# A graph layer on one core: other weights for the dense steps when they are dealt over the groups

## The chip, the cores and the metric

The kernel runs on one core of a Trainium2 chip. The metric is device time in microseconds (us), a median over runs; a profile of one execution stands beside it. TensorE (PE) multiplies, VectorE (DVE) and ScalarE (ACT) work elementwise, GpSimd (POOL) issues the indirect DMAs that gather rows, SyncE (SP) issues the plain DMAs.

## What is computed

The reference, cut to what matters:

```python
def reference(x, src, dst, edge_type_4, W, b):      # x 12500x128, 200000 edges, W 4x128x128
    h = jnp.maximum(layernorm(x), 0.0)
    xs = h[src]
    msgs = zeros
    for i in range(4):
        msgs += jnp.where(edge_type == i, xs @ W[i] + b[i], 0.0)
    return x + jax.ops.segment_sum(msgs, dst, num_segments=12500)
```

The edges come sorted by `dst`, and the low nodes have many more edges than the high ones.

## The kernel before

The edges are taken in chunks of 128. The first 568 chunks (`C0`), whose nodes have many edges, are the **dense part**; the rest is the **grouped part**, groups of 16 chunks (`G`), numbered from 0, 65 in all.

*Preparation.* The table of normalised rows, each as three 16-bit parts (768 bytes), is written to `htab` in device memory. Meanwhile the first three groups (`RAW = 3`, the "raw groups") gather rows of x itself, since the table isn't there yet, and normalise them on ScalarE.

*A group of the grouped part* (3 and up). POOL gathers the rows of each chunk from `htab` (`gather`, L591), two chunks to a buffer `hm`, ten buffers. VectorE makes a one-hot matrix of each chunk (`one_hots_of`, L609). `sum_up` multiplies rows by one-hots (L644), a pair of chunks, called a part, at a time, eight parts to a group; ScalarE evicts the sums (L634). `weigh` multiplies by the weights (L670) in the second part of the next group, and VectorE adds the result to a ring of output columns (`ring_adds`, L733).

*The dense part* has 19 batches of up to 31 units of three nodes. `count` counts, for each batch, how often each table row goes to each node: one matmul of two one-hot matrices for each slot (L1099), 1069 slots in all; VectorE makes both one-hots (L1066, L1074), ScalarE casts the result to integers (L1107). `multiply` then passes the whole table by those counts, 33 steps of three blocks of 128 rows: a load of `hs` by SP, and matmuls (L1211). The first batch's pass reads `htab`, uses all three parts of a row (nine matmuls a step), and writes the rows again, in a shorter form, to `dtab` (`keep`, L1181 and L1182, stores from ScalarE's queue). The later passes read `dtab` and have six matmuls a step; three of them take counts that ScalarE has decoded to floats (L1167). While one batch is passed, the next one is counted. Two stretches of counting stand alone: that of the first batch, where there is nothing to pass yet, and the first half of the third one's (`SETTLE = 0.5`), which goes ahead of the second batch's pass.

*The order.* From group 3 on, the order on TensorE, VectorE and ScalarE is the program's own. Ahead of each part of a group, the loop pulls steps from the generator `dense_work` until the share of dense work done, `spent`, has reached what is due by then:

```python
while work and spent < pace(gi, part):
    spent = next(work, None)
```

`pace` wants groups of equal length: each group, from 3 to 58, gets the same number of columns in all, its own (`columns`) and dense ones. `dense_columns` is the sum of dense columns that it reckons with, and `dense_work` has a weight for each batch's counting and pass, from which it works out `spent`. In both, a node of a pass costs `PARTS` = 2.05 times 392 columns, in the first pass 3.0 times. A slot is 392 columns; in the first batch `dense_work` makes it 3.5 times that, `dense_columns` does not. In the first of the groups from 3 on the 20 steps of the raw groups' products stand as well (`raw_steps`), which no column count has in it.

Of the kernel before, what the change touches and what calls it, by code (L numbers as in the profile page):

```python
# [66 lines left out]
SETTLE = 0.5  # L67
# [5 lines left out]
LEAD = RAW  # L73
# [4 lines left out]
DECS = 4  # L78
UP = 4096.0
PARTS = 2.05  # L80


@with_exitstack
def kernel(
# [13 lines left out]
    NT, _, DO = w.shape  # L98
    assert D == P and DO == P
    NW = -(-N // P)  # L100
# [19 lines left out]
    def chunks_of(d, n):  # L120

        m = E * (((d + n) / N) ** 0.5 - (d / N) ** 0.5)
        return max(1, -(-int(m + ODDS * m**0.5) // P))
# [18 lines left out]
    for k in range(max(segs[0][4])):  # L142
        for s in (0, 1, 2, 3) if k == 0 else (1, 0, 2, 3):
            n = sum(c > k for c in segs[s][4])
# [11 lines left out]
    def window_of(c):  # L156

        m = min((c - C0) // G, FULL)
        end = (C0 + (m + 1) * G if m < FULL else T) * P / E
        a_node = E * ((end**2 + 1 / N) ** 0.5 - end)  # L160
        return next((n for n in range(8, WIN, 2) if (n - 1) * a_node > P + 5 * P**0.5), WIN)
# [6 lines left out]
    alone = [(k, d) for k in range(0, max(segs[0][4]), 2) for d in range(FIRST) if segs[0][4][d] > k]  # L168
# [10 lines left out]
    batches = []  # L179
# [11 lines left out]
    def slot_at(k, d):  # L191
        s = next(s for s in (3, 2, 1, 0) if d >= segs[s][2])
        return blocks[k, s][0] + (d - segs[s][2]) // segs[s][3]

    def slots_of(u):

        got = []
        u = list(zip(u, (1.0, 256.0, 65536.0)))
        if u[0][0] is not None and u[0][0][1] >= FIRST:
            d = u[0][0][1]  # L200
            size = size_of(d)
            got += [(slot_at(k, d), None) for k in range(chunks_of(d, size))]
            del u[:size]
        for v, by in u:
            if v is not None:
                k, d = v
                got += [(slot_at(i, d), by) for i in (k, k + 1) if i < segs[0][4][d]]
        return got

    NSLOTS = sum(len(slots_of(u)) for vs in batches for u in vs)  # L210
    NB = NW * NT
# [132 lines left out]
    def prep_steps(m, prep):  # L344
        c0, c1 = C0 + m * P, min(C0 + (m + 1) * P, T)
        got = []
        for name, of, rest in (("si", src, 0), ("ty", etype, NT), ("di", dst, N - 1)):
            t = prep.tile([P, 1, P], I32, name=name)
            edge_rows(t, of, c0, c1, rest)
            got.append(t)  # L350
        load_brow(m)
        si, ty, di = got
        if c1 > NFULL and REST:
            r = (NFULL - c0) % P
            nc.sync.dma_start(di[r : r + 1, 0, REST:], dst[E - (P - REST) :].rearrange("(p e) -> p e", p=1))
        yield 0
        sf = prep.tile([P, 1, P], F32, name="sf")
        nc.vector.tensor_copy(sf, si)
        nc.vector.tensor_copy(head[:, m : m + 1], di[:, :, 0])
        rel = prep.tile([P, 1, P], F32, name="si")  # L360
        nc.vector.tensor_scalar(rel[:, 0, :], di[:, 0, :], head[:, m : m + 1], None, ALU.subtract)
        key = prep.tile([P, 1, P], F32, name="di")
        nc.vector.scalar_tensor_tensor(
            key[:, 0, :], ty[:, 0, :], span[:, m : m + 1], rel[:, 0, :], op0=ALU.mult, op1=ALU.add
        )
        nc.vector.tensor_reduce(ends[:, m : m + 1, 0], rel, AX.X, ALU.max)
        nc.vector.tensor_sub(ends[:, m : m + 1, 0], ends[:, m : m + 1, 0], span[:, m : m + 1])
        nc.vector.tensor_reduce(ends[:, m : m + 1, 1], rel, AX.X, ALU.min)
        yield 1
        settle(owed)  # L370
        pg = x_ps.tile([P, 2, P], F32, name="pt")
        nc.tensor.transpose(pg[:, 0, :], sf[:, 0, :], ident)
        nc.tensor.transpose(pg[:, 1, :], key[:, 0, :], ident)
        nc.scalar.copy(srcT[:, m % TURN, :], pg[:, 0, :])
        nc.scalar.copy(keyT[:, m % TURN, :], pg[:, 1, :])
# [240 lines left out]
    def settle(of):  # L616
        while of:
            of.pop(0)()
# [642 lines left out]
    def columns(gi):  # L1261

        K = NT * window_of(C0 + starts[gi])
        return sizes[gi] * (3 * max(64, K) + 5 * K)

    def pace(gi, part):

        last = FULL - 1
        if gi >= last:
            return 2.0  # L1270
        own = [columns(i) for i in range(LEAD, last)]
        a_group = (dense_columns() + sum(own)) / len(own)
        n = gi - LEAD
        if n < 0:
            return 0.0
        return ((n + part) * a_group - sum(own[:n]) - part * own[n]) / dense_columns()

    def dense_columns():
        return NSLOTS * float(NB) + sum(3 * len(vs) * (PARTS if i else 3.0) for i, vs in enumerate(batches)) * NW * NT

    def begin(n):
        now = [batches[n], None]
        return now, count(now, lambda: rooms[n % 2])

    def dense_work():


        a_slot = float(NB)
        alone_slot = 3.5 * NB
        a_node = NW * NT  # L1290
        total = dense_columns() + sum(len(slots_of(u)) for u in batches[0]) * (alone_slot - a_slot)
        gone = 0.0
        before = None
        coming = None
        for n, vs in enumerate(batches + [None]):
            steps, led = {}, {}
            now = None
            if n == 1:
                end_raws()
            if vs:  # L1300
                now, first = coming or begin(n)
                coming = None
                steps[first] = sum(len(slots_of(u)) for u in vs) * (a_slot if before else alone_slot)
            if before:
                passed = multiply(before)
                steps[passed] = 3 * len(before[0]) * a_node * (PARTS if before[0] is not batches[0] else 3.0)
                led = {passed: SETTLE if before[0] is batches[1] else BEHIND}
            done = {st: 0.0 for st in steps}
            opened = 0 if before else DECS - 1
            while done:  # L1310
                while opened < DECS - 1 and (
                    vs is None or done.get(first, 1.0) >= led[passed] - BEHIND * (DECS - 1 - opened) / (DECS - 1)
                ):
                    next(passed)
                    opened += 1
                st = min(done, key=lambda st: done[st] + led.get(st, 0.0))
                part = next(st, None)
                if part is None:
                    del done[st]
                    gone += steps[st]  # L1320
                    if vs and st is first and n + 1 < len(batches):
                        coming = begin(n + 1)
                        next(coming[1])
                else:
                    done[st] = part
                    yield (gone + sum(done[st] * steps[st] for st in done)) / total
            before = now
        settle(sds)

# [98 lines left out]
    for gi, us in enumerate(group_of):  # L1428
# [9 lines left out]
        for i, u in enumerate(us):  # L1438
# [7 lines left out]
            last = None  # L1446
            for l in more_looks[:each]:
                last = l()
# [50 lines left out]
    def end_raws():  # L1499

        while raw_steps:
            raw_steps.pop(0)()
        if len(rooms) > 1:
            return
        raw_sums = outp.tile([P, OT, D], F32, name="xo").rearrange("p j d -> p (j d)")[:, : raw_at[-1]]
        nc.scalar.copy(raw_sums, raw_py[:, : raw_at[-1]])
        for m in range(RAW):
            win = window_of(C0 + m * G)
            of = lambda i, m=m, win=win: raw_sums[:, raw_at[m] + i * win : raw_at[m] + (i + 1) * win]
            raw_adds.append(ring_adds(m * G, G, of, win))  # L1510
        raw_room.close()
        rooms.append(counting.enter_context(tc.tile_pool(name="dense2", bufs=1)))
        rooms.append(counting.enter_context(tc.tile_pool(name="hsp", bufs=STREAM, side="right")))

    work = dense_work()

    gates.extend(ties + marks[len(marks) - (20 - 1 - len(ties)) :])

    steps = [prep_steps(1, later)]
# [11 lines left out]
    for gi, (t0, g) in list(enumerate(zip(starts, sizes)))[RAW:]:  # L1531
        q = (t0 + 8 * G) // P
        if (t0 + 8 * G) % P < G and 2 <= q < BM:
            steps = [prep_steps(q, later)]
# [17 lines left out]
        for j, part in enumerate(sum_up(t0, g, *now, gi >= FULL)):  # L1552
            late, tails[:] = list(tails), []
            while work and spent < pace(gi, part):
                spent = next(work, None)
                if spent is None:
                    work = None
# [80 lines left out]
    with tc.If(rv > 0):  # L1638
        with tc.tile_pool(name="slow", bufs=1) as slow, tc.tile_pool(name="slow_ps", bufs=1, space=PSUM) as slow_ps:
# [10 lines left out]
            before = slow.tile([P, P], F32, name="before")  # L1650
# [108 lines left out]
```

## Time and profile before

| | |
|---|---|
| median of 3 runs | 1355.36 us (1352.13 to 1356.22) |
| the profiled execution | 1360.44 us |
| its span | 1358.7 us |
| PE busy | 1243.1 us (91%) |
| ACT busy | 1066.8 us (79%) |
| DVE busy | 999.0 us (74%) |
| POOL busy | 977.8 us (72%) |
| gathers by POOL (L591) | 947, mean 976 ns |

In the rows of the prediction, a group of instructions reads: line, engine, operation, out<-in, count, busy time and mean ns of one, idle time before them and what ended it. A row by stretches has the stretch, then busy time and count of each engine, then TensorE's granted clock, the busy share of the DMA engines, and GB/s. A wait reads: who waited, for whom, us in total, times, the longest.

### The profile page before, as it was taken

The page shows a single profiled execution, that of the slowest core. Times are in us where ns is not written, and L with a number is a line of the kernel's source. Part 1 is how long each engine was busy: PE and PEld are TensorE (multiplying, and loading weights), DVE is VectorE, ACT ScalarE, POOL GpSimd, SP SyncE. Part 2 cuts the span into 40 slices and gives each one's busy share as a digit, 9 for nine tenths or more (in the row PEclk, how much of TensorE's full clock was granted, in tenths as well). Part 3 has the DMA queues.
Part 4 walks back from the last instruction along what each step waited for, and adds up shares of the span by engine and source line. Part 5 has one row for each costly group of instructions (what it writes and reads, how often), then busy time and mean ns, then how long its engine had stood idle before and what let it go on. Part 6 is the DMA issues. An engine that isn't in the chain of part 4 may idle for free.

```text
span 1358.7 us, 30461 instructions
## 1 busy us (share of the span) xinstructions
PE 1243.1 (91%) x9232; PEld 872.8 (64%) x9232; DVE 999.0 (74%) x5139; ACT 1066.8 (79%) x1815; POOL 977.8 (72%) x1024
## 2 busy tenths in 40 slices
PE   5888877999999999999999999999999999998964
PEld 1445654777677766777777676666676666666743
DVE  8996568868888897888776867677676758773552
ACT  6887544889889888898988988888897978886710
POOL 7637463777777777777777777777777777777774
PEclk8885887999999999999999999999999999999977
DMA  7653596888788888888888888887877878778842
GB/s 243 216 204 86 176 338 216 244 272 266 243 256 259 250 255 241 249 257 265 256 259 254 267 249 257 248 246 246 273 227 238 265 214 261 235 234 281 267 122 62
DMA packets 184630, 322.56 MB, mean 237 GB/s; under 512 B 30243, under 2 KB 82524, under 8 KB 184460
## 3 DMA queue, kind: packets, MB, share of 16 engines
q1 hardware_dynamic: 132716, 214.63, 49.0%
q0 software_dynamic: 46992, 96.30, 26.0%
q10 hardware_dynamic: 4752, 9.64, 1.8%
q8 instruction: 73, 1.20, 0.4%
q14 instruction: 97, 0.79, 0.2%
HBM read 294.78 MB, written 25.67 MB: 236 GB/s over the span
## 4 chain that ended last, share of the span: by engine, by line
PE 65%; DMA 12%; DVE 6%; ACT 6%; issue 6%; POOL 4%; DVEq 0%; SPq 0%; ACTq 0%; POOLq 0%
PE pa L1211 35%; PE pt L1099 9%; PE py L670 7%; DMA hm<-htab,srcT 7%; PE ps L644 5%; POOL hm L591 4%; DMA dtab<-dec 2%; DMA hs<-dtab 2%; ACT dec L1167 2%; PE pt L1235 2%; ACT counts L1107 1%; PE ps L702 1%; DVE o L1074 1%; DVE o L1066 1%; PE pt L952 1%
## 5 line engine op out<-in xcount | busy, mean ns | idle before, releaser
L591 POOL DMA_INDIRECT hm<-htab,srcT x947 | 924.3, 976 | 342.1 <-issue 202.5
L1167 ACT ACTIVATE dec<-counts 128x1116 fp32r<-128x1116 uint8 (+1 forms) x594 | 672.2, 1152 | 9.9 <-PE pa L1211 9.0
L1066 DVE TENSOR_SCALAR o<-iota_n,hkT 128x392 bf16<-128x392 f16 x1069 | 354.4, 331 | 180.2 <-PE pt L1099 177.4
L1211 PE MATMUL pa<-dec,hs 128*128 128x372 f32 x1764 | 480.8, 380 | 0.0
L1211 PE MATMUL pa<-counts,hs 128*128 128x372 fp8e4 (+1 forms) x2058 | 435.0, 324 | 22.6 <-DMA hs<-htab 13.8
L1211 PEld LDWEIGHTS pa<-dec,hs 128*128 128x128 f32 x1764 | 309.5, 188 | 41.6 <-issue 0.5
L1107 ACT CAST counts<-pt 128x396 int32<-128x396 f32 x580 | 285.5, 510 | 50.1 <-PE pt L1099 26.2
L1099 PE MATMUL pt<-o,o 128*128 128x396 bf16 x1069 | 285.9, 342 | 15.8 <-ACT counts L1107 9.5
L1211 PEld LDWEIGHTS <-hs 128*128 128x128 f16 (+1 forms) x2058 | 189.6, 98 | 143.1 <-issue 19.4
L644 PE MATMUL ps<-oh,hm 128*128 128x72 bf16 (+7 forms) x2841 | 186.9, 201 | 32.3 <-DMA hm<-htab,srcT 30.9
L1074 DVE TENSOR_SCALAR o<-iota,loT,byT 128x128 bf16<-128x128 bf16 x647 | 216.3, 334 | 0.0
L733 DVE TENSOR_TENSOR ring<-ring,py 128x18 f32 (+6 forms) x912 | 159.0, 174 | 73.1 <-PE py L670 24.1
L644 PEld LDWEIGHTS <-hm 128*128 128x128 f16 x2841 | 136.9, 100 | 103.9 <-DMA hm<-htab,srcT 41.4
L634 ACT ACTIVATE sb<-ps 128x288 f32<-128x288 f32 (+8 forms) x237 | 101.8, 430 | 126.3 <-PE py L670 101.3
L609 DVE TENSOR_SCALAR oh<-iota_b,keyT 128x72 bf16<-128x72 bf16 (+7 forms) x947 | 163.0, 260 | 25.6 <-PE ps L644 24.4
L670 PE MATMUL py<-sb,wsb 128*128 128x288 f32 (+6 forms) x456 | 121.1, 409 | 0.0
L1099 PEld LDWEIGHTS <-o 128*128 128x128 bf16 x1069 | 80.4, 99 | 60.6 <-issue 17.5
L1074 DVE TENSOR_SCALAR o<-iota,loT 128x128 bf16<-128x128 bf16 x422 | 116.7, 277 | 0.0
L670 PEld LDWEIGHTS py<-sb,wsb 128*128 128x128 f32 x456 | 83.3, 193 | 20.7 <-issue 0.3
L575 POOL DMA_INDIRECT hx<-in_x_dram,srcT x48 | 48.0, 1001 | 23.8 <-issue 9.5
L665 ACT CAST cnt<-pt 128x288 bf16<-128x288 f32 (+10 forms) x62 | 25.5, 412 | 39.5 <-PE pt L661 33.6
L509 ACT ACTIVATE h<-hm,nmrt,rstdt 128x128 f32<-128x128 f32 x98 | 42.1, 489 | 0.9 <-DVE mvt L492 0.8
(250 smaller groups left out, 717.8 us busy)
## 6 DMA issues: line engine op xcount, KB each, us to landing
hs<-dtab SPq DMA_DIRECT2D x576, 288.0 KB
hm<-htab,srcT POOLq DMA_INDIRECT x947
htab<-h SPq DMA_DIRECT2D x32, 288.0 KB
hs<-htab SPq DMA_DIRECT2D x32, 288.0 KB
dtab<-dec ACTq DMA_DIRECT2D x32, 288.0 KB
xo<-in_x_dram SPq DMA_DIRECT2D x23, 256.0 KB
out_dram<-xo SPq DMA_DIRECT2D x23, 256.0 KB
hm<-in_x_dram SPq DMA_DIRECT2D x18, 192.0 KB
```

The source lines that it names most:

```text
L591: one = nc.gpsimd.indirect_dma_start(out=hm[:, (i - h0) * D3 : (i - h0 + 1) * D3], out_offset=None, in_=htab, in_offset=bass.IndirectOffse ...
L609: nc.vector.tensor_scalar(oh[:, i, :], iota_b[:, :K], keyf[:, at : at + 1], None, ALU.is_equal)
L634: nc.scalar.activation(sb[0][:, i0:i1].rearrange("p g t n -> p g (t n)"), ps[:, : i1 - i0, :], AF.Copy, scale=1.0 / UP)
L644: nc.tensor.matmul(ps[:, i - i0, :], rows(i, c), oh[:, i, :], start=(c == 0), stop=(c == 2))
L670: nc.tensor.matmul(py[:, :g, :], wsb[:, t, :], sb[0][:, :g, t, :], start=False, stop=(t == NT - 1))
L733: nc.vector.tensor_tensor(to, to, of(i), ALU.add)
L1066: one = nc.vector.tensor_scalar(o2[:, k, :NB], iota_n, hkT[:, s : s + 1], None, ALU.is_equal)
L1074: one = nc.vector.tensor_scalar(o1[:, k], iota_1, loT[:, s : s + 1], by, ALU.is_equal, ALU.mult)
L1099: one = nc.tensor.matmul(pb, o1, o2, start=first, stop=last)
L1107: lambda i=i, pb=pb: nc.scalar.copy(counts[:, :, i * NT : (i + 1) * NT], pb.rearrange("p (b t) -> p b t", t=NT))
L1167: nc.scalar.activation(decoded[n][:, : j1 - j0, :nv].rearrange("p j (m v) -> p j m v", m=3), by_digit[:, j0:j1, : nu * NT * 4].rearrange(" ...
L1211: nc.tensor.matmul(to if c == 1 and not first else to.rearrange("p (m v) -> p m v", m=3), left, right, start=(j == 0 and c == 0), stop=(js ...
```

## The change

Three weights are added, and the same functions now give them to `pace` and to `dense_work`. A slot that is counted alone is charged `ALONE` = 3.5 times its columns, in the first batch and in the first half of the third, in both places. A node of the first pass is charged 4.4 times 392 columns in place of 3.0. The first group of the loop is charged 20000 columns on top of its own, some 6900, for the raw groups' products. The sum of dense columns goes from 1841890 to 1933481. What is computed, and by which instructions, stays as it is: only the places at which dense steps are pulled move.

```diff
+FIRST_PASS = 4.4
+ALONE = 3.5
+RAW_WORK = 20000.0
...
-        own = [columns(i) for i in range(LEAD, last)]
+        own = [columns(i) + (RAW_WORK if i == LEAD else 0.0) for i in range(LEAD, last)]
         a_group = (dense_columns() + sum(own)) / len(own)
...
+    def counting_columns(n, part):
+        alone = 1.0 if n == 0 else SETTLE if n == 2 else 0.0
+        return sum(len(slots_of(u)) for u in batches[n]) * NB * (part + (ALONE - 1.0) * min(part, alone))
+
+    def passing_columns(n, part):
+        return 3.0 * len(batches[n]) * (PARTS if n else FIRST_PASS) * NW * NT * part
+
     def dense_columns():
-        return NSLOTS * float(NB) + sum(3 * len(vs) * (PARTS if i else 3.0) for i, vs in enumerate(batches)) * NW * NT
+        return sum(counting_columns(n, 1.0) + passing_columns(n, 1.0) for n in range(len(batches)))
...
-        a_slot = float(NB)
-        alone_slot = 3.5 * NB
-        a_node = NW * NT
-        total = dense_columns() + sum(len(slots_of(u)) for u in batches[0]) * (alone_slot - a_slot)
+        total = dense_columns()
...
-                steps[first] = sum(len(slots_of(u)) for u in vs) * (a_slot if before else alone_slot)
+                steps[first] = lambda part, n=n: counting_columns(n, part)
...
-                steps[passed] = 3 * len(before[0]) * a_node * (PARTS if before[0] is not batches[0] else 3.0)
+                steps[passed] = lambda part, n=n: passing_columns(n - 1, part)
...
-                    yield (gone + sum(done[st] * steps[st] for st in done)) / total
+                    yield (gone + sum(steps[st](done[st]) for st in done)) / total
```

More of the change, by code (lines that the diff above doesn't have):

```diff
@@ L1319, in dense_work @@
                     del done[st]
-                    gone += steps[st]
+                    gone += steps[st](1.0)
                     if vs and st is first and n + 1 < len(batches):
```

## The prediction

> **What bounds the kernel now.** I read the page first, then the stretches of the span by engine, then the waits of POOL in two windows, then TensorE's timeline for the places where each group's result is made.
>
> ```profile
> PE 1243.1 (91%) x9232; PEld 872.8 (64%) x9232; DVE 999.0 (74%) x5139; ACT 1066.8 (79%) x1815; POOL 977.8 (72%) x1024
> L591 POOL DMA_INDIRECT hm<-htab,srcT x947 | 924.3, 976 | 342.1 <-issue 202.5
> ```
>
> The 947 gathers of the table's rows all go through POOL, and "issue" before them is no wait for anything. POOL's gathers by stretch (POOL busy with count, granted clock, DMA share, GB/s), then its waits from 250 to 1225 us (first two rows) and from 100 to 250 us (last three; us in total, times, longest):
>
> ```profile
> 95.00:245.00 150.00, 87.28 (x85) 0.74 0.62 203
> 245.00:1345.00 1100.00, 836.99 (x863) 0.98 0.81 246
> 1289.00:1345.00 56.00, 42.39 (x45) 0.71 0.40 106
> POOL hm L591 <- issue: 161.9, 531, 0.3
> POOL hm L591 <- PE pt L1099: 18.0, 59, 0.3
> ...
> POOL hm L591 <- PE ps L644: 25.1, 10, 5.0
> POOL hm L591 <- PE pt L1099: 12.4, 9, 3.4
> POOL hm L591 <- ACT sb L634: 5.7, 1, 5.7
> ```
>
> From 245 us on POOL issues without a stop: 1100 / 863 = 1.275 us a gather, no wait over 0.3 us; 16 gathers of a group make 20.4 us. Before 245 us it issued 85 gathers in 150 us, which at 1.275 would have taken 108: there it stood still for 42 us, blocked by buffers that TensorE had not freed. So POOL sets the end, but the time was lost early. TensorE is hardly less full (columns: PE, PEld, DVE, ACT, POOL, clock, DMA share, GB/s):
>
> ```profile
> 112.00:152.00 40.00, 33.32 (x200) 25.66 (x200) 21.41 (x96) 30.36 (x84) 23.69 (x25) 0.63 0.26 72
> 152.00:184.00 32.00, 24.47 (x221) 18.33 (x220) 23.01 (x104) 15.09 (x37) 19.34 (x19) 0.87 0.94 321
> 184.00:212.00 28.00, 22.81 (x206) 16.58 (x203) 17.84 (x79) 12.26 (x29) 17.24 (x18) 0.96 0.97 329
> 212.00:238.00 26.00, 19.24 (x102) 10.29 (x103) 23.48 (x113) 13.57 (x28) 9.07 (x9) 0.66 0.54 179
> 286.10:730.00 443.90, 435.00 (x3472) 315.26 (x3470) 363.99 (x1894) 393.78 (x623) 338.41 (x347) 1.00 0.84 253
> 730.00:1289.00 559.00, 536.73 (x4063) 382.13 (x4062) 390.32 (x2037) 467.53 (x712) 424.86 (x441) 1.00 0.82 251
> PE ps L644 <- DMA hm<-htab,srcT: 12.0, 21, 2.5
> ```
>
> The last row is a wait from 730 to 1290 us. From 286 to 730 us TensorE idles 8.9 us of 444 (2.0%) and never for a gathered row: it is the bound there, and POOL's lead of up to 20 gathers (ten buffers of two) is used up. From 730 on it idles 4.0%, 12 us of it for rows: POOL leads no more. Three early stretches are worse: 152 to 212 us has the DMA engines at 94 to 97%, 212 to 238 us has VectorE at 23.5 of 26 us with TensorE at 0.66 of its clock. The groups' ends (the product with the weights, made in the second pair of the next group; the first five are rows of TensorE's timeline with start and length, the sixth of the chain) show it:
>
> ```profile
> 156.21 1.49 PE L670 MATMUL py<-sb,wsb 128*128 128x192 f32 x8
> 187.01 1.49 PE L670 MATMUL py<-sb,wsb 128*128 128x192 f32 x8
> 215.42 2.17 PE L670 MATMUL py<-sb,wsb 128*128 128x192 f32 x8
> 247.70 1.49 PE L670 MATMUL py<-sb,wsb 128*128 128x192 f32 x8
> 266.57 1.49 PE L670 MATMUL py<-sb,wsb 128*128 128x192 f32 x8
> 286.11 1.34 PE py L670 x8
> ```
>
> Groups 3 to 8 end there: groups 4, 5 and 6 take 30.8, 28.4 and 32.3 us against POOL's 20.4; 7 and 8 take 18.9 and 19.5.
>
> **The change part by part.** No instruction is added or removed; only which slot countings ("counts", L1099) and which products of three node blocks ("steps", L1211) stand in which group. Counted in the two programs:
>
> ```
> group            3   4   5   6   7   8  | 9-28   29-55  (mean)
> counts before   29  12  13  41  24   4  | 22.8   18.1
> counts after    14  19   9  10  10  27  | 23.2   18.9
> steps  before    2  13  13   8  12  15  | 11.35  11.0
> steps  after     0   6  10  10   7   0  | 12.0   11.6
> ```
>
> At the end of group 8 the kernel is 34 counts and 30 steps further behind than before. All first-pass steps (33) are done by then in both. Prices (timeline rows of TensorE; group rows of VectorE; DMA):
>
> ```profile
> 206.97 2.60 PE L1211 MATMUL pa<-counts,hs 128*128 128x264 fp8e4 x18
> 249.35 0.66 PE L1211 MATMUL pa<-counts,hs 128*128 128x372 fp8e4 x3
> 250.36 0.51 PE L1099 MATMUL pt<-o,o 128*128 128x396 bf16 x2
> 250.71 0.66 PE L1211 MATMUL pa<-counts,hs 128*128 128x372 fp8e4 x3
> L1066 DVE TENSOR_SCALAR o<-iota_n,hkT 128x392 bf16<-128x392 f16 x1069 | 354.4, 331 | 180.2 <-PE pt L1099 177.4
> L1074 DVE TENSOR_SCALAR o<-iota,loT,byT 128x128 bf16<-128x128 bf16 x647 | 216.3, 334 | 0.0
> L609 DVE TENSOR_SCALAR oh<-iota_b,keyT 128x72 bf16<-128x72 bf16 (+7 forms) x947 | 163.0, 260 | 25.6 <-PE ps L644 24.4
> L733 DVE TENSOR_TENSOR ring<-ring,py 128x18 f32 (+6 forms) x912 | 159.0, 174 | 73.1 <-PE py L670 24.1
> q0 software_dynamic: 46992, 96.30, 26.0%
> dtab<-dec ACTq DMA_DIRECT2D x32, 288.0 KB
> ```
>
> A later step is 250.36 - 249.35 = 1.01 us of TensorE, a count (250.71 - 250.36) / 2 = 0.175 (twice that at half clock), a first-pass step about 1.25 (18 matmuls in 2.60, the last ending late). A count costs VectorE 0.331 + some 0.31 = 0.64 us. A first-pass step reads 288 KB and writes 288 KB, 0.59 MB; a group's gathers (the q0 row: packets, MB) are at most 16 x 96.3 MB / 947 = 1.6 MB.
>
> *Group 3.* Ahead of its end stand 21 counts in place of 32 and no step in place of 5. At the clock of that stretch (0.63, half of it at 0.5) that is 11 x 0.35 + 5 x 1.25 = 10 us of TensorE, which is busy 33 of 40 us there; I take 9 (4 if the raw groups' own chain holds). End at 147.
>
> *Groups 4 to 6.* In the stretches 152 to 212 us a step and its share of gathers ran at 321 to 329 GB/s. Between the ends lie now 9, 9 and 10 steps in place of 13: 9 x 0.59 + 1.6 = 6.9 MB is 21 us, 10 make 22.8. VectorE in the first: 16 counts 10.2, one-hots and ring adds 16 x (0.26 + 0.17) = 6.9, 16 raw ring adds 2.8, nine additions for the stores at 0.56 (33 in 18.0 us, the L1182 group) 5.0: 25 us, less what is made ahead. I take 24, 21.5 and 22.5.
>
> ```profile
> L1182 DVE TENSOR_TENSOR dec<-hs 128x384 fp32r<-128x384 bf16 (+1 forms) x33 | 18.0, 553 | 14.4 <-ACT dec L1181 14.4
> ```
>
> *Groups 7 and 8.* The first pass ends in 7 (20 us, about POOL's rate). Group 8 counts alone: 26 counts between the ends are 16.6 us of VectorE, 7 for one-hots and ring, 1 for flushing: 24.6, less slots made ahead: 23 us, with TensorE mostly idle. The clock pays for that:
>
> ```profile
> 231.00:236.00 5.00, 3.76 (x13) 1.37 (x11) 5.00 (x26) 4.63 (x8) 1.67 (x2) 0.50 0.15 39
> 239.00:242.00 3.00, 3.00 (x22) 2.80 (x21) 2.01 (x14) 2.62 (x4) 1.62 (x3) 0.72 0.65 166
> ```
>
> In the old place of this counting it is at 0.50, and it comes back some 5 us after the steps do: 2 to 3 us lost, in either place once, so nothing in the difference. The Trainium skill, "TensorE: Matmul & The Clock Gate", section on the HAM clock gate, speaks against a group of bare counting: idle windows of about 3.4 us halve the clock, and about as long a busy stretch restores it. By its figure the return would cost an estimated 1.7 us rather than 2 to 3; the trace agrees in kind (0.50, then 0.72).
>
> Sum: 147 + 24 + 21.5 + 22.5 + 20 + 23 = 258 us for the end of group 8, 28 earlier than 286.1; from 247 to 270 with each term at its ends.
>
> *After group 8.* TensorE was busy 435.0 + 536.7 = 971.7 us from there to the last step at 1289. To this come 30 x 1.01 + 34 x 0.175 = 36.3: 1008 us. At the idle share of the stretch where it was the bound (2.0%) that is 1029 us, 20.6 a group against POOL's 20.4. The waits for rows go, and TensorE is late next, all the way; the last step is at 258 + 1029 = 1287, hardly sooner than now. POOL however then stands at its full lead: at 258 us TensorE has used 100 gathers (six groups and two pairs of the next), POOL can have issued 120, and 800 more take 1020 us, to 1278, ahead of 1287.
>
> *The end.* At 1289 us 45 gathers were still to come: POOL had issued 902, and TensorE had used 900 (56 groups and two pairs). With 20 ahead there remain 27 at 56 / 45 = 1.25 us: 34 us in place of 56, 22 us saved. The span runs on 14 us behind the last gather in both.
>
> ```profile
> 1343.85 0.94 POOL L591 DMA_INDIRECT hm<-htab,srcT  x1 [0.30 <-issue]
> ```
>
> So the span of 1358.7 becomes 1287 + 34 + 14 = 1335, minus 24. The profiled execution took 1360.44 us, 5 above the median of the three runs (1355.36); 24 off that median is 1331.
>
> **The rivals.** *POOL stays the bound from the start.* If the early groups end by 247 us and TensorE idles under 1.2%, the last gather is bounded by POOL: 120 issued at 247, 827 x 1.275 more, to 1301, span 1315, 1311 on the median's scale. For it: no wait of POOL for 1100 us. Against it: 36 us more of TensorE work in a stretch with 31 idle. 0.12.
>
> *Half of it is eaten.* TensorE idles 2.5 to 3.5% where it is the bound, as the fuller groups collide with batch changes: 1008 / 0.975 = 1034 to 1008 / 0.965 = 1045 in place of 1029; or the early end falls at 270. By the same sum 1336 to 1347. For it: the stretch from 730 us on, where 10 us of idle (1.8%) are left when the waits for rows are taken off, and batches still end every third group. 0.20.
>
> *No change to speak of.* Both of these at once: 270 + 1008 / 0.97 = 1309, a span of 1357, and 1353 on the median's scale. That the steps aren't moved is excluded by the table. 0.06.
>
> *Slower: ScalarE becomes the bound.* It decodes one 1.15 us block for each step and casts 0.5 us for each pair of counts, on one queue, and TensorE waits for both.
>
> ```profile
> L1107 ACT CAST counts<-pt 128x396 int32<-128x396 f32 x580 | 285.5, 510 | 50.1 <-PE pt L1099 26.2
> L1167 ACT ACTIVATE dec<-counts 128x1116 fp32r<-128x1116 uint8 (+1 forms) x594 | 672.2, 1152 | 9.9 <-PE pa L1211 9.0
> PE pt L1099 <- ACT counts L1107: 3.3, 5, 0.9
> ```
>
> From 286 to 730 us it is busy 394 of 444 us (89%), and the groups there get 0.65 steps more (6%): 93 to 94%. From an idle share of TensorE of 4.3% on the change loses: 1008 / 0.95 = 1061 gives a last step at 1319, a span of 1367, 1363 on the median's scale. Against it: the wait that would show it (last row, 286 to 730 us) is 3.3 us in total. 0.07.
>
> **How the numbers follow.** My forecast, 1331 with its own range of 1320 to 1339, has 0.55. The range 1311 to 1352 takes in the first two rivals and leaves out some 0.15 to 0.2: the same, the slower and the edge of the POOL case. 0.3% (4 us) is about what can be told from no change. Faster 0.87, same 0.06, slower 0.07.
>
> **What would show it.** Right: group 8's weight product near 258 us; the groups 4 to 6 at 21 to 24 us each; POOL waiting for "PE ps L644" again after 300 us, in stops of more than 0.3 us; TensorE without waits for rows until about 1290; from there to the end some 48 us in place of 70. Wrong: ends of groups 4 to 6 still 28 us apart, or TensorE's waits for "ACT dec" and "ACT counts" grown to tens of us, or a last step well after 1300 us.

## The result, and the profile after

The changed kernel takes 1339.2 us in the median of four runs (1335.5 to 1340.7), the kernel before 1355.0 beside it; the ratio is 0.9876, with an interval of 0.9852 to 0.9900. A second set on another chip gave 0.9904 (0.9875 to 0.9933). The forecast was 1331 in a range of 1311 to 1352.

The profiled execution took 1337.9 us, with a span of 1336.2. First POOL's gathers, by the same stretches as before (POOL busy with count, clock, DMA share, GB/s; the last one runs from the last step to the end):

```profile
L594 POOL DMA_INDIRECT hm<-htab,srcT x947 | 921.7, 973 | 324.3 <-issue 214.2
95.00:245.00 150.00, 104.64 (x105) 0.72 0.64 208
245.00:1345.00 1100.00, 815.17 (x842) 0.99 0.80 245
1278.80:1336.20 57.40, 33.03 (x35) 0.81 0.36 95
1321.24 0.95 POOL L594 DMA_INDIRECT hm<-htab,srcT  x1 [0.30 <-issue]
```

By 245 us POOL has issued 105 gathers in place of 85, and its last one goes out at 1321.2 in place of 1343.9. Those 20 gathers, at 1.275 us each, are 25 us; 22.7 of them are still there at the end. (In the second set's profile its last gather goes out at 1326.7, so there it is 17.) The groups' ends (TensorE's timeline, rows of the product with the weights) and the early stretches by engine (PE, PEld, DVE, ACT, POOL, clock, DMA share, GB/s):

```profile
148.52 1.49 PE L673 MATMUL py<-sb,wsb 128*128 128x192 f32 x8
170.31 1.49 PE L673 MATMUL py<-sb,wsb 128*128 128x192 f32 x8
190.14 1.49 PE L673 MATMUL py<-sb,wsb 128*128 128x192 f32 x8
220.15 2.52 PE L673 MATMUL py<-sb,wsb 128*128 128x192 f32 x8
239.20 2.82 PE L673 MATMUL py<-sb,wsb 128*128 128x192 f32 x8
260.53 1.49 PE L673 MATMUL py<-sb,wsb 128*128 128x192 f32 x8
...
152.00:184.00 32.00, 25.00 (x226) 17.77 (x226) 26.54 (x127) 14.86 (x36) 24.69 (x25) 0.90 0.84 275
212.00:238.00 26.00, 15.05 (x126) 10.54 (x125) 17.09 (x80) 8.95 (x23) 17.60 (x18) 0.76 0.92 319
238.00:262.00 24.00, 18.40 (x136) 13.31 (x137) 23.18 (x129) 13.86 (x25) 18.20 (x20) 0.83 0.42 113
```

Groups 4 and 5 now take 21.8 and 19.8 us, 7 and 8 take 19.1 and 21.3. Group 6 still takes 30.0: two stalls, 6.0 us for a block of the table and 4.5 us until VectorE had made the ring adds and one-hots that stand ahead of the output block:

```profile
196.11 0.66 PE L769 MATMUL pt<-ident,ring 128*128 128x128 f32 x2 [4.48 <-DVE oh L612]
218.03 2.16 PE L1214 MATMUL pa<-counts,hs 128*128 128x264 fp8e4 x9 [6.03 <-DMA hs<-htab]
```

From the end of group 8 on, and POOL's waits from 290 to 1279 us:

```profile
261.00:1278.80 1017.80, 1000.44 (x7730) 719.66 (x7728) 767.52 (x3998) 893.21 (x1375) 769.83 (x795) 1.00 0.84 258
POOL hm L594 <- issue: 173.7, 570, 0.3
POOL hm L594 <- PE pt L1102: 20.2, 64, 1.0
POOL hm L594 <- PE ps L647: 18.1, 43, 1.6
```

TensorE idles 17 us of 1018 (1.7%; 3.1% before), and its matmuls never wait for a gathered row in that stretch (its weight loads do for 2.4 us in all, 0.2 the longest). POOL now waits for TensorE at times (1.0 and 1.6 us the longest), where none of its waits after 245 us was over 0.3 us before the change.

### The profile page after: what moved, and what is told of

Its sections match the earlier page's. It is cut to its first block, busy times and chain, and to the rows that moved or that the text cites. A ratio compares the mean times of both kernels' runs of the same rounds, so it can differ in the third digit from the quotient of the medians.

```text
span 1336.2 us, 30461 instructions
## 1 busy us (share of the span) xinstructions
PE 1232.2 (92%) x9232; PEld 873.9 (65%) x9232; DVE 996.9 (75%) x5139; ACT 1064.3 (80%) x1815; POOL 974.9 (73%) x1024
## 5 line engine op out<-in xcount | busy, mean ns | idle before, releaser
L1214 PE MATMUL pa<-counts,hs 128*128 128x372 fp8e4 (+1 forms) x2058 | 435.2, 325 | 21.8 <-DMA hs<-htab 12.2
L1110 ACT CAST counts<-pt 128x396 int32<-128x396 f32 x580 | 289.4, 518 | 56.4 <-PE pt L1102 26.8
L1077 DVE TENSOR_SCALAR o<-iota,loT,byT 128x128 bf16<-128x128 bf16 x647 | 220.7, 341 | 0.0
L647 PE MATMUL ps<-oh,hm 128*128 128x72 bf16 (+7 forms) x2841 | 178.6, 200 | 6.6 <-DMA hm<-htab,srcT 6.3
L647 PEld LDWEIGHTS <-hm 128*128 128x128 f16 x2841 | 137.9, 100 | 70.5 <-issue 19.6
L1077 DVE TENSOR_SCALAR o<-iota,loT 128x128 bf16<-128x128 bf16 x422 | 113.1, 268 | 0.0
```

Of the source, the lines that this page charges most:

```text
L647: nc.tensor.matmul(ps[:, i - i0, :], rows(i, c), oh[:, i, :], start=(c == 0), stop=(c == 2))
L1077: one = nc.vector.tensor_scalar(o1[:, k], iota_1, loT[:, s : s + 1], by, ALU.is_equal, ALU.mult)
L1110: lambda i=i, pb=pb: nc.scalar.copy(counts[:, :, i * NT : (i + 1) * NT], pb.rearrange("p (b t) -> p b t", t=NT))
L1214: nc.tensor.matmul(to if c == 1 and not first else to.rearrange("p (m v) -> p m v", m=3), left, right, start=(j == 0 and c == 0), stop=(js ...
```

## Experiments

Theory P says that POOL sets the end, theory T that TensorE does, B that the two are tied. Times are medians; "of before" is the ratio to the kernel before on the same chip.

**Each weight alone.** The edits:

```diff
 # e1: the first pass's weight alone (kernel before)
-(PARTS if i else 3.0)   and   (PARTS if before[0] is not batches[0] else 3.0)
+(PARTS if i else 4.4)   and   (PARTS if before[0] is not batches[0] else 4.4)
 # e2: standing alone, alone (changed kernel)
-FIRST_PASS = 4.4
-RAW_WORK = 20000.0
+FIRST_PASS = 3.0
+RAW_WORK = 0.0
 # e3: the raw groups alone (kernel before)
-own = [columns(i) for i in range(LEAD, last)]
+own = [columns(i) + (20000.0 if i == LEAD else 0.0) for i in range(LEAD, last)]
```

> Of the three weights only the first pass's changes (4.4 in place of 3.0, in both places). Counted in the program: groups 3 to 8 have 29, 9, 9, 7, 42, 25 counts and 2, 9, 9, 10, 7, 12 steps. Theory P (POOL sets the end: from the end of group 8 on it issues without a stop, so the span ends some 1072 us after group 8's weight product, at whatever TensorE has left to do): groups 4 to 6 take 22 us each, 7 takes 32, 8 takes 20, the end of group 8 lies at 274 us in place of 286, the time is 10 to 15 us under the kernel before, 1340 to 1345. Theory T (TensorE sets the end; POOL only follows, with its full lead of 20 gathers): 14 more steps than before are left after group 8, 1006 us from 274, the last step at 1280 and 48 us behind it: a span of 1328, 1322 to 1330 on the median's scale.

> Only counting that stands alone is charged 3.5 times, in both places; first pass 3.0, nothing for the raw groups. Counted: groups 3 to 8 have 29, 12, 13, 19, 24, 26 counts and 2, 13, 13, 5, 5, 12 steps: groups 3 to 5 are those of the kernel before. Theory P: group 6 takes 22 us in place of 32, 7 takes 23, 8 takes 21, the end of group 8 lies at 281 in place of 286: 3 to 8 us faster, 1347 to 1352. Theory T: 13 more steps left after group 8, 1005 us from 281 and 48: a span of 1334, 1328 to 1334 in the median.

> Only the 20000 columns of the raw groups are charged to the first group. Counted: groups 3 to 8 have 13, 22, 12, 18, 41, 17 counts and 0, 8, 13, 12, 9, 13 steps. Theory P: the end of group 3 comes at 148 as in the changed kernel, then 24, 28, 27, 32 and 20 us: the end of group 8 at 280, 3 to 8 us faster, 1347 to 1352. Theory T: 8 more steps left, 1000 us from 280 and 48: a span of 1328, 1322 to 1330 in the median. With P the gains of the three single weights add up to about the whole one (16 us); with T each alone would give more than the whole.

Measured: e1 1342.7, 0.9876 of before (0.9849 to 0.9904); e2 1348.5, 0.9922 (0.9902 to 0.9942); e3 1358.6, 0.9997 (0.9979 to 1.0016); the kernel before was at 1359.6 on this chip, about 4 us above the others. So 17, 11 and 1 us. The first pass's weight alone gives as much as all three. Theory T had all three at 20 us and more; e3 rules it out for these versions, and e2 speaks against it. P had 10 to 15 us for e1 and 3 to 8 us for e2 and e3: e1 and e2 are better than that and e3 worse, and the single gains do not add up (29 us, against 16 for the whole). What P names can be counted in each trace: gathers by 245 us, the end of group 8 (its product with the weights), the time of the last gather, and what runs from the end of group 8 to the end of the span (one profiled execution each).

| kernel | gathers by 245 us | end of group 8, us | last gather, us | end of group 8 to end of span, us |
|---|---|---|---|---|
| before | 85 | 286.1 | 1343.9 | 1072.6 |
| e3, raw groups | 88 | 285.2 | 1340.8 | 1070.8 |
| e2, standing alone | 93 | 272.3 | 1327.0 | 1070.5 |
| e1, first pass | 96 | 273.4 | 1327.4 | 1068.8 |
| changed | 105 | 260.5 | 1321.2 | 1075.7 |
| changed, second set | 104 | 262.1 | 1326.7 | 1079.8 |

POOL's waits from 290 us to the last step: two rows of e1, then the longest in the second profile of the changed kernel:

```profile
POOL hm L591 <- issue: 152.4, 500, 0.3
POOL hm L591 <- PE ps L644: 12.2, 40, 0.3
POOL hm L594 <- PE ps L647: 21.3, 44, 2.2
```

In e1, e2 and e3, as before the change, POOL has no wait over 0.3 us there, and the span ends 1069 to 1073 us after group 8, as P has it (1072). So P's rule holds for these three versions; what its forecasts had wrong for e2 and e3 is where group 8 ends (281 and 280 us expected). Up to there the single gains do nearly add up: 12.7, 13.8 and 0.9 us, against 25.6 and 24.0 for the whole. With all three weights POOL is made to wait again, and the rest takes 1076 to 1080 us, 3 to 7 us more than before the change: that much of the early gain is lost.

**Less work for TensorE, or for POOL.** First some products of the later passes are left out:

```diff
-                    if not first:
+                    if not first and j % 12:
                         todo.append((1, j, ... decoded ...))
```

> The changed kernel, without the second product (decoded counts by the bf16 half of the row) for 9 of the 98 node blocks in each of the 18 later passes: 162 matmuls of about 0.155 us, 25 us less work on TensorE, spread evenly; loads, decoding and gathers as they were. Theory P: POOL still issues 947 gathers at 1.277 us, so 0 to 5 us under the changed kernel: 1334 to 1339. Theory T: the 25 us come off, 1312 to 1318.

Measured: 1335.6 us, 0.9828 of before (0.9808 to 0.9847), against 0.9876 and 0.9904 for the changed kernel: some 6 to 10 us for 25 us of TensorE, a little over P's 0 to 5 and far from T's 21 to 27. The last step and the end by TensorE's stretches, the gathers behind the last step, and TensorE's wait there:

```profile
261.00:1256.70 995.70, 972.48 (x7524) 689.78 (x7522) 763.00 (x3979) 887.44 (x1369) 757.88 (x781) 1.00 0.85 261
1256.70:1328.00 71.30, 43.92 (x47) 0.75 0.34 92
PE ps L647 <- DMA hm<-htab,srcT: 21.4, 26, 1.8
```

The last step did come 22 us earlier, but 47 gathers were still to be issued then, and TensorE waits for them: with TensorE relieved, POOL sets the end. That was half of it. The other half leaves out gathers:

```diff
             for i in range(h0, min(h0 + HG, g)):
+                if g == G and i == G - 1:
+                    continue
 ...
-        return lambda i, c: of(got[i // HG], c)[:, (i % HG * 3 + c) * D : (i % HG * 3 + c + 1) * D]
+        in_hm = lambda i: 0 if g == G and i == G - 1 else i % HG
+        return lambda i, c: of(got[i // HG], c)[:, (in_hm(i) * 3 + c) * D : (in_hm(i) * 3 + c + 1) * D]
```

> The changed kernel once more, beside the following ones on the same chip: 0.985 to 0.990 of the kernel before.

> The changed kernel, without the gather of the sixteenth chunk of each full group (its products use the fifteenth's rows): 57 gathers fewer, 73 us less of POOL's queue, TensorE's work as it was. Theory P in its plain form (POOL sets the end and TensorE has room): 55 to 75 us come off. Theory T (TensorE sets the end): only the lead at the last step grows from 12 to 20 gathers, 10 us. Theory B (the two are tied: TensorE idles 1.7% after group 8 and can give back at most 17 us before it is the bound): the last step moves from 1279 to 1262 to 1272, the lead is full, and 20 to 32 us come off in all: 1307 to 1320.

Measured: 1339.4 us, 0.9885 (0.9861 to 0.9910), beside 1342.5 us and 0.9904 (just outside what was expected of it) for the changed kernel: nothing that can be told apart, for 73 us less of POOL's queue. Its stretch behind group 8, POOL's longest waits there, and the gathers behind the last step:

```profile
261.00:1279.20 1018.20, 1001.29 (x7731) 720.13 (x7729) 764.18 (x3988) 892.94 (x1375) 720.35 (x744) 1.00 0.83 253
POOL hm L596 <- PE ps L650: 64.4, 67, 3.0
POOL hm L596 <- PE pt L1105: 44.3, 79, 2.0
1279.20:1334.00 54.80, 31.64 (x34) 0.83 0.36 97
```

POOL now has time over in which it waits for TensorE, and the last step does not move: T holds for the changed kernel up to there. B's 17 us of idle time were not to be had: TensorE idles 1.7% with or without, and what it waits for isn't rows: in the changed kernel 12 of the 17 us are waits for ScalarE, 2.7 for loads of the passes, 2.2 for VectorE. Nor did the lead grow. Behind the last step 50 gathers had yet to be used in this kernel, 34 had yet to be issued: a lead of 16, though POOL's last wait for TensorE had ended 10 us before (1.0 us long, at 1268.6). Ten buffers of two are worth 16, not 20, at that place, and the changed kernel has those 16 already (51 and 35).

**Both at once, and the same omission before the change.** The last two edits together, and the second one in the kernel before:

> The changed kernel with both omissions at once: 162 products of the passes fewer (25 us of TensorE) and 57 gathers fewer (73 us of POOL). Alone they moved the changed kernel by about 6 and 3 us. Theory B (TensorE and POOL are tied after group 8, each is the bound as soon as the other is relieved): together far more than the sum of 9 us: the last step moves from 1279 to about 1255, the lead at it stays the full 16 gathers, 20 to 26 us come off: 0.970 to 0.976 of the kernel before. If something third (ScalarE, DMA) is the bound: no more than 10 us off, 0.982 to 0.986.

> The kernel before the change, without the gather of the sixteenth chunk of each full group: 57 gathers fewer. Theory: before the change POOL alone was the bound after 250 us, TensorE idled 3.1% from group 8 to the last step. So here the omission pays, which brought the changed kernel 3 us only: TensorE's idle share falls to 1.8%, 13 us earlier at the last step, and the lead there grows from 6 to 16 gathers, 12 us: 20 to 25 us off, 0.982 to 0.986 of the kernel before. If TensorE was the bound before as well: 0 to 8 us off, 0.994 to 1.

Measured: both together 1314.0 us, 0.969 (0.9668 to 0.9712), 25 to 29 us under the changed kernel by the ratios; in the kernel before 1329.3 us, 0.9798 (0.9771 to 0.9824), 26 us off; both are a little more than was expected with TensorE and POOL tied. The stretches from 261 us to the last step, of e8 and then of e9, each followed by the gathers behind it:

```profile
261.00:1257.60 996.60, 974.77 (x7552) 691.68 (x7551) 765.23 (x3994) 890.47 (x1374) 720.69 (x744) 1.00 0.84 258
1257.60:1313.00 55.40, 31.91 (x34) 0.81 0.36 96
```

```profile
261.00:1271.70 1010.70, 989.07 (x7705) 712.23 (x7703) 759.24 (x3984) 878.05 (x1357) 738.82 (x764) 1.00 0.83 253
1271.70:1328.00 56.30, 31.94 (x34) 0.81 0.36 95
```

That settles which two engines it is. Before the change POOL was the bound: 57 gathers fewer are worth 26 us there. After it TensorE sets the last step and POOL the stretch behind it, so that relieving one alone brings 0 to 10 us and both together 25 and more. ScalarE as the bound would have kept e8 from moving. The DMA engines have 57 gathers less to carry in e8 and e9 too, so these two runs do not rule them out; POOL's rate does: a gather took 1.275 us before the change with the DMA engines 81% busy, and still 1.25 us in the last stretch, at 40%. And e9 is faster than e5 (0.9798 against 0.9885, intervals apart): with fewer gathers the old order is the better one, its last step comes at 1271.7, not 1279.2. The change buys POOL's time with TensorE's.

**More lead.** 12 buffers for the rows and, for room, 4 for the passes' loads:

```diff
-    hpool = mid.enter_context(tc.tile_pool(name="rows", bufs=10))
+    hpool = mid.enter_context(tc.tile_pool(name="rows", bufs=12))
-STREAM = 5
+STREAM = 4
```

> The changed kernel with 12 buffers of two gathers in place of 10, and, as they wouldn't fit otherwise, 4 buffers for the loads of the passes in place of 5. Theory P: POOL's standstills ahead of 245 us shrink by four gathers once, 2 to 6 us faster than the changed kernel. Theory T: no more than 2 us. Against both: if the passes miss the fifth load ahead, some us slower in the first pass.

Measured: 1364.1 us, 1.0074 (1.0046 to 1.0102), 22 us slower than the changed kernel. TensorE's waits between 290 us and the last step at 1310.7 (first its matmuls, then its weight loads):

```profile
PE pa L1214 <- DMA hs<-dtab: 21.0, 27, 2.8
PEld L1214 <- DMA hs<-dtab: 35.0, 49, 3.1
```

The changed kernel has 5.0 and 7.2 us there in its second set. The fifth load ahead is missed, and in the later passes, where I had not looked for it. The longer lead does shorten what runs behind the last step, from 57.4 to 51.3 us with 30 gathers to come in place of 35, but the last step comes 26 us later. Two sizes changed at once, so what more lead alone would give stays open.

**Without the raw groups' charge.** `RAW_WORK = 0.0` in the changed kernel, in two sets, and with `FIRST_PASS = 5.2` as well:

> The changed kernel without the charge of 20000 columns for the raw groups (first pass 4.4, standing alone 3.5 in both places). Counted: groups 3 to 8 have 29, 9, 9, 7, 21, 25 counts and 2, 9, 10, 10, 2, 6 steps. Theory P: the end of group 3 at 156 as before the change, then 22, 22, 22, 21 and 22: the end of group 8 at 265 in place of 260: 3 to 6 us slower than the changed kernel, as fast as with the first pass's weight alone or up to 7 us faster. If the raw groups' charge brings nothing (as it did alone), it is as fast as the changed kernel.

> The changed kernel without the raw groups' charge once more, in five rounds: 0.985 to 0.990 of the kernel before, that is the changed kernel's time or up to 5 us under it.

> The changed kernel without the raw groups' charge and with 5.2 in place of 4.4 for the first pass. Groups 3 to 8 have 29, 8, 7, 9, 8, 28 counts and 2, 8, 8, 9, 6, 0 steps. If early standstills of POOL still cost something: the groups 4 to 6 at 20 us each, 3 to 6 us under the kernel without the raw groups' charge. If TensorE is the bound after group 8: the same within 3 us, since as much work is only left for later.

Measured: 1337.6 us, 0.9881 (0.9842 to 0.9920), beside the changed kernel's 1342.5; 1338.0, 0.9865 (0.9843 to 0.9888); with 5.2, 1342.1, 0.9891 (0.9864 to 0.9917). The charge for the raw groups brings nothing: without it group 3 ends at 155.7 in place of 149.5 us, but by the end of group 6 the two are 2.8 us apart (223.9 and 221.1). The version without it is the one with the lowest medians among those that leave out no work, yet its lead over the changed kernel is within the intervals. More weight on the first pass gives nothing more (4 us above the version with 4.4, inside the intervals), as it should where TensorE is the bound after group 8: the last step of that version is at 1284.1, with TensorE 98.1% busy from 261 us on.

## Why the prediction held, and where it was off

*What bounds it.* POOL before the change, time lost early: shown by e9 and by the count of gathers. TensorE after it up to the last step: shown by e5. It is a near tie: in the changed kernel no wait of POOL from 290 us to the last step is over 2.2 us. That most of the gain comes from POOL's lead behind the last step is seen in the traces: 6 gathers before, 16 after, and 70.3 us from last step to end become 57.4. In the second profile they are 57.4 as well, while the last step comes only 3.9 us earlier than before the change (1284.5 and 1288.4), not 9.6 as in the first.

*Early groups.* Forecast ends 147, 171, 192.5, 215, 235, 258; measured 148.5, 170.3, 190.1, 220.2, 239.2, 260.5. The sum was right to 2.5 us, its parts not: group 6 took 7.5 us more than forecast, the groups 4, 5, 7 and 8 together 6.5 us less, and that these cancel is luck. I costed each group of the first pass at the DMA rate of its own steps. Five of the 33 loads had been issued by 92.3 us, so groups 4 and 5 ran ahead on blocks loaded before, and group 6 paid with a wait of 6.0 us; its other stall, 4.5 us for VectorE, has no term in the sum.

*After group 8.* Forecast: 1008 us of TensorE at 2.0% idle, last step at 1287. Measured 1000.4 at 1.7%, 1278.8. The work moved behind group 8 came out as 29 us (1000.4 less 971.2 before), not 36. The two traces show where most of the other 7 are. At the place of group 8's weight product 28.7 steps and 32 counts more are left than before (the prediction's 30 and 34 hold for the end of group 8's own parts, a little earlier), at its prices 34.6 us; and the products of the gathered rows (L644, L647) in that stretch, 2392 in both, are busy 148.3 us in place of 152.9. The prediction put no change there.

*The end.* This step failed: a full lead of 20 gathers, 22 us saved, and some 48 us left behind the last step. I took TensorE to have used 900 at the last step, but the two pairs of group 59 come behind it: 896, so the lead before was 6, not 2; and the full lead at that place is 16, not 20. Saved: 10 gathers, 12.9 us. The two errors, 8 us early at the last step and 9 late behind it, cancel by luck: span 1335 forecast, 1336.2 measured. Of the prediction's signs of being right, these 48 us and group 6's 21 to 24 us were missed, and group 5 is 1.2 us under that range; group 4, group 8's end, POOL's waits for TensorE and, up to the last step, TensorE without waits for rows came as said.

*From span to median.* The 24 us were taken off the median, as if the second profile stood to its median as the first. The first was 5 us above its own, the second 1 below: 22.5 us between the spans, 16 between the medians. A second profile of the changed kernel had a span of 1341.9. That is the larger part of the 8 us that the forecast is off by.

*The rivals.* The median, 1339.2, lies at the upper edge of the forecast's own range and inside that of the rival by which half of the gain is eaten (1336 to 1347), but not for that rival's reasons: TensorE idles 1.7%, not 2.5 to 3.5, and group 8 ends at 260.5 us, not 270. POOL is not the bound from the start either: the early groups do not end by 247 us. ScalarE did not become the bound: TensorE's waits for its casts from 290 to 730 us are 3.6 us in total (3.3 before). Bare counting lowers the granted clock in either place: the stretch of the counting, 238 to 262 us, is at 0.83, its old place at 0.66; there it is at 0.50 from 231 to 236 us although TensorE is busy for 3.76 of these 5 us. What that costs no run shows by itself.

## What to carry to other kernels

When two engines are both near full, ask of each change which one it gives time to and which one pays: here an order that spares POOL early leaves TensorE more for later, and the gain ends where TensorE becomes the bound. Relieve each engine alone and then both together; if little moves but for both, the two are tied. Count a queue's lead in the trace, at the place where it matters, and compare medians with medians: one profile can stand 5 us off its own.

## What the runs showed of the hardware

POOL issues a gather of 128 rows of 768 bytes each 0.95 us with 0.30 between: 1.25 to 1.28 us from 245 us to the end before the change (1043 us for 818 up to the last step, 56 us for 45 behind it), whether the DMA engines are 83% or 40% busy. Taking one of five load buffers from the passes (and giving the gathers two) cost 22 us, with the DMA engines 83% busy in the stretch: TensorE's matmuls waited 21 us for `hs` in place of 5.
